# Attention scores as products of 32 rows on four quarters of the array, in place of stacked products fed by copies

## The chip, the core and the metric

The kernel runs on one core of one Trainium2 chip. The time is the device time of one execution in microseconds (us), as the median of three runs. The core has a matrix engine (TensorE, PE in the profile; its weight loads are a row of their own, PEld), a vector engine (DVE), a scalar engine (ACT), a general engine (POOL), and SP, which mostly issues DMAs. Matrix products go to PSUM, which the kernel uses as eight banks of 512 float32 values on each of 128 partitions. The program gives each engine one row of instructions, in the order of the text described below.

## The reference

Two layers of a transformer on `x` of 2 batches x 1024 tokens x 256 channels, with a context of 64 rows per batch. After each layernorm there is a residual step:

```
x += xattn0(ln(x), ctx)   # 16 heads of 16 channels; q, k, v; softmax over the 64 keys; then relu MLP 256-512-256
x += ffn0(ln(x), ...)     # 8 experts, top 2: relu(x wi + bi + low-rank term of the expert), then wo
x += xattn1(ln(x), ctx)   # one head
x += ffn1(ln(x), ...)     # linear
```

The change is in the first attention alone: `scores = q k / 4`, softmax over the 64 keys, for 16 heads.

## The kernel before

The 2048 tokens are cut into eight halves (n = 0 to 7) of 256 tokens, which stay in SBUF. Every piece of work on a half is a generator ("stream"): `q`n makes the queries, `a`n the scores and exponentials, `v`n the product with the values, `m` the MLP, `e`, `d` and `t` the head, the upper and the lower product of the experts, and `o`n the second layer. `m`, `e` and `d` go by blocks of one or two halves (`BLOCKS`). Other streams load and scale the weights (`ld`, `sk`, `ky`, `w0` and so on), and `pe` issues products of zeros that nobody reads. One long text, `ORDER`, lists the steps: each token advances its stream to the next `yield`, and so fixes the order on every engine. A "!" behind a token sets `other[0]`, which lets the helpers (`copy`, `times`, `plus`, `relu`, `two`) take VectorE in place of ScalarE or GpSimd for that step.

Float32 precision is reached by splitting an operand into two float16 parts, high and low, and adding three products: high by high, high by low, low by high (`mm3`, L187).

A half's attention before the change. `att_q` turns the normalised tokens, multiplies them by the query weights, and leaves `qT`, high and low, with the channels on 128 partitions: 8 heads of 16 channels in each of two chunks c. Three DMAs (L540) copy `qT` into `qp`, so that on 96 partitions a pair of heads has its high part, its low part and its high part again below each other; there are four pairs per chunk. The keys lie in `kp` in the same way (high, high, low; L369). One product over 96 rows thus adds all three terms. `att` first makes the scores with tokens on partitions (L557: 16 products of 128 columns a half, each four of them one bank) and takes the largest value of each head on VectorE (L564, four instructions). L571, L574 and L576 subtract a constant and split the maxima into two float16 parts, L579 turns them, `copy` moves them to SBUF, and a DMA (L584) puts them as four more rows into `qp`. The second product (L595, 8 of 256 columns) runs over 100 rows, with keys on partitions, and so yields the scores less their maximum. ScalarE takes the exponential twice (L603 in float32 and L607 in float16; with "!" VectorE copies instead, L605), and `two` (L171) makes the low part. `att_out` (L624) multiplies by the values.

PSUM is one pool of eight banks for all streams (`p_tile`); SBUF scratch tiles come in three sizes, 4, 2 and 1 KB per partition, with the counts in `SLOTS`.

## Time and profile before

| what | value |
|---|---|
| median of three runs | 313.85 us (312.57 to 315.66) |
| the profiled execution: its time, its span | 314.17 us, 312.2 us |
| PE busy | 284.8 us (91%), 2504 products |
| DVE busy | 260.0 us (83%), 774 instructions |
| ACT, POOL busy | 155.8 us (50%), 162.8 us (52%) |
| DMA | 25.38 MB in 53324 packets |
| first product L557; first and last product L595 | at 36.2 us; at 49.7 and 134.1 us |
| first product of the experts (`xT` by `wi`) | at 115.3 us |

The span runs from the first to the last instruction of the program; the time is taken around it, 1.97 us more here. A row of the profile names line, engine, operation and tiles, then busy time, mean duration, and the idle time of the engine ahead of it. The durations of neighbouring products overlap in the timeline; so the distance from start to start, not the duration, says what a product takes of the engine.

### The profile page before, as it was taken

Reading aid. Unit: us, or ns where it says so; the run is one execution under the profiler, and the core shown is the slowest. Engines: PE = TensorE matmul, PEld = TensorE weight load, DVE = VectorE, ACT = ScalarE, POOL = GpSimd, SP = SyncE. Lnnn points to the kernel's source line nnn. Section 1 sums busy time; section 2 is a strip of 40 time slices with the busy share of each in tenths; the row PEclk is TensorE's granted clock in tenths of the full one; section 3 lists DMA queues with packets and bytes.
Section 4 is the critical chain, followed back from the end, with each engine's and each line's share of the span. In section 5 each row is a group of like instructions: output and inputs, shape, how many; then the busy total and the mean of one; then the engine's idle time right before and its main releaser. Section 6 shows DMA issues by size and latency. Waiting matters only on the chain. (4 is left out here: it accounts for less than half of the span.)

```text
span 312.2 us, 6880 instructions
## 1 busy us (share of the span) xinstructions
PE 284.8 (91%) x2504; PEld 208.9 (67%) x2504; DVE 260.0 (83%) x774; ACT 155.8 (50%) x347; POOL 162.8 (52%) x211
## 2 busy tenths in 40 slices
PE   8799979887969799999989989999998999989785
PEld 2455648675958378886876856547765788878563
DVE  3759997999968999995998799699688879979685
ACT  1686486986867855468123531230436244253251
POOL 3583384797765657644624534240735643545441
PEclk9699987998988999999999999999999999999799
DMA  7996988245230013313133203210033121224844
GB/s 249 351 323 154 206 133 118 41 93 50 55 69 2 4 34 38 69 34 69 32 64 59 52 1 72 41 34 11 0 36 76 37 42 36 42 44 95 119 120 149
DMA packets 53324, 25.38 MB, mean 81 GB/s; under 512 B 44838, under 2 KB 49702, under 8 KB 53292
## 3 DMA queue, kind: packets, MB, share of 16 engines
q1 hardware_dynamic: 52732, 24.17, 37.6%
q10 hardware_dynamic: 560, 0.79, 0.8%
q8 instruction: 19, 0.31, 0.4%
q14 instruction: 13, 0.11, 0.1%
HBM read 8.50 MB, written 2.10 MB: 34 GB/s over the span
## 5 line engine op out<-in xcount | busy, mean ns | idle before, releaser
L187 PEld LDWEIGHTS <-h 128*128 128x128 f16 x576 | 54.6, 98 | 11.8 <-issue 2.1
L171 POOL TENSOR_TENSOR h<-r,h 128x256 f16<-128x256 f32 (+1 forms) x33 | 27.4, 830 | 50.9 <-DVE h L148 23.9
L187 PE MATMUL n<-wo_h,h 128*128 128x256 f16 x256 | 44.7, 273 | 0.7 <-POOL h L171 0.7
L187 PE MATMUL n<-uT,lb_h 128*128 128x256 f16 (+1 forms) x192 | 42.3, 308 | 2.4 <-DVE r L166 1.2
L187 PE MATMUL n<-xT,wi_h 128*128 128x256 f16 (+1 forms) x192 | 41.6, 308 | 1.0 <-DVE r L822 0.6
L171 POOL TENSOR_TENSOR e<-e,e 128x512 f16<-128x512 f32 x27 | 31.5, 1171 | 10.1 <-DVE e L605 5.2
L187 PE MATMUL n<-wo_l,h 128*128 128x256 f16 x128 | 34.9, 273 | 0.0
L168 ACT ACTIVATE r<-n,cols 128x256 f32<-128x256 f32 (+1 forms) x33 | 18.0, 548 | 26.1 <-PE n L187 24.7
L171 POOL TENSOR_TENSOR x<-xn,x 128x512 f16<-128x512 f32 x19 | 22.9, 1208 | 15.0 <-ACT x L150 8.7
L187 PE MATMUL n<-xT,wi_l 128*128 128x256 f16 (+1 forms) x96 | 29.6, 308 | 0.0
L187 PE MATMUL n<-uT,lb_l 128*128 128x256 f16 (+1 forms) x96 | 29.6, 308 | 0.0
L199 DVE BATCH_NORM_STATS2 stats<-x 128x6 f32<-128x256 f32 x64 | 24.8, 415 | 4.6 <-DMA x<-in_x_dram 4.3
L150 ACT CAST h<-r 128x256 f16<-128x256 f32 (+1 forms) x21 | 9.7, 463 | 36.8 <-DVE r L822 36.8
L822 DVE SCALAR_TENSOR_TENSOR r<-n,nbi,r 128x256 f32<-128x256 f32 (+1 forms) x48 | 27.0, 564 | 0.7 <-PE n L187 0.7
L206 POOL TENSOR_TENSOR rstd<-rstd,mhalf 128x2 f32<-128x2 f32 (+2 forms) x32 | 22.9, 717 | 6.6 <-DVE rstd L205 4.5
L187 PEld LDWEIGHTS <-lb_h 128*128 128x128 f16 x192 | 18.6, 98 | 11.3 <-issue 3.8
L248 ACT ACTIVATE xn<-x,nm,rstd 128x256 f32<-128x256 f32 x28 | 15.3, 592 | 21.0 <-DVE nm L244 18.3
L1131 PE MATMUL n<-warm 128*128 128x512 f16 x80 | 24.3, 457 | 1.2 <-DVE warm L1135 1.2
L564 DVE TENSOR_REDUCE mm<-n 128x8 f32<-128x512 f32 x32 | 22.1, 690 | 3.7 <-PE n L557 2.2
L187 PEld LDWEIGHTS <-wi_h 128*128 128x128 f16 x192 | 18.4, 98 | 9.0 <-issue 0.8
L187 PE MATMUL n<-aw_h,h 128*128 128x256 f16 x128 | 22.9, 273 | 1.2 <-DVE h L171 1.1
L603 ACT ACTIVATE e<-n,sinv 128x512 f32<-128x512 f32 x32 | 22.0, 690 | 3.0 <-PE n L595 2.6
(260 smaller groups left out, 702.2 us busy)
## 6 DMA issues: line engine op xcount, KB each, us to landing
qp<-qT SPq DMA_DIRECT2D x24, 128.0 KB, 4.3
x<-in_x_dram SPq DMA_DIRECT2D x7, 256.0 KB, 4.7
out_dram<-x SPq DMA_DIRECT2D x7, 256.0 KB, 2.4
raw<-in_aw_dram SPq DMA_DIRECT2D x2, 512.0 KB
raw<-in_wo_dram SPq DMA_DIRECT2D x2, 512.0 KB, 8.1
raw<-in_wi_dram SPq DMA_DIRECT2D x2, 512.0 KB
raw<-in_lb_dram SPq DMA_DIRECT2D x1, 512.0 KB
cw<-in_cw_dram SPq DMA_DIRECT2D x2, 256.0 KB, 5.4
```

Source lines behind the costliest of these rows:

```text
L150: s.copy(dst, src)
L168: s.activation(dst, src, AF.Relu, bias=bias)
L171: (v if other[0] else g).tensor_tensor(dst, x, y, op)
L187: nc.tensor.matmul(pm, lhsT=x, rhs=y, start=start and i == 0, stop=stop and i == 2, skip_group_check=True,)
L199: v.bn_stats(stats[:, t, :], xt)
L206: g.tensor_tensor(rs, rs, mhalf[:, 0:k], ALU.pow)
L248: s.activation(xn[:, t], xt, AF.Identity, bias=nm[:, t : t + 1], scale=rstd[:, at + t : at + t + 1])
L564: v.tensor_reduce(mx[:, :, :, c, t].rearrange("q j p -> q p j"), pm.rearrange("q (p j m) -> q p j m", j=2, m=M), AX.X, ALU.max,)
L603: s.activation(e, pm, AF.Exp, scale=sinv)
L822: v.scalar_tensor_tensor(r1, pa, nbi[:, f : f + 1], r1, ALU.max, ALU.add)
L1131: nc.tensor.matmul(pm, lhsT=warm[:, 0:P], rhs=warm, start=True, stop=True)
```

## The change

The copies between partitions go. Each quarter of the array (32 rows) now holds one pair of heads as `qT` already has it, and the three terms are three products that add up in PSUM.

- `att_q` ends with `qT`; the three copies into `qp` are gone, and so are the three copies into `kp`.
- The keys are two tiles `kd` (high and low) on the same partitions as `qT`; for each of the two heads of a pair the other head's channels are zeroed by multiplying with a mask (`heads`, a column of the input).
- First pass: 48 products of 32 rows and 128 columns a half, in two steps. Four neighbours in the order go to four quarters and four banks. Four maxima instructions follow, one per bank.
- The maxima are split into the tile `ms`, one of two that stay and are zeroed once; the subtraction of the constant is gone, and the exponential gets it as a bias (`raised`).
- Two transposes in place of one, one copy `mT`, no DMA.
- Second pass: 24 products of 32 rows and 256 columns into four banks (one per pair, both chunks), in two steps, then 8 more with a fixed selection matrix `sel` that subtract the maxima. Exponentials as before, one pair of heads and both chunks each.
- `SLOTS` changes, and `ORDER` is a new text: 1500 steps in place of 1548, which is five fewer for each `a` and one fewer for each `q`; every other stream has as many steps as before, in other places and with "!" at other places.

```diff
--- before.py
+++ after.py
@@ -41,12 +41,8 @@
 HTOP = 2.0**15
 USC = 2.0**-8
 MROW = 2048.0
-STOP = 2.0**25
 DMIN = -87.3365
-
-PK = 3 * 32
-PKS = PK + 4
-SHIFT = 40.0
+SHIFT = 10.0
 
 BLOCKS = ((0,), (1,), (2, 3), (4, 5), (6,), (7,))
 
@@ -59,51 +55,50 @@
 
 
 ORDER = """
-l2 ky st pe pe pe q2 q2 q2 l4 q4 q4 q4 q4 l3 q3 l0 pe pe pe pe pe l7! lq ld ld! sk ld sc sc q3 q3 q7 q3! l1 pe
-pe pe pe q7 w0 sk sk pe q0 sk st q7 q7 q4! q0 pe q4 w0 q0 q0 q7! q7 sc sc q0! q1 wq q1 q1 l5 q5 q5 q5 lv q0 q1
...
+st l0! pe q0 q0 q0 l7! q7 q0! q7 q7 l3! q3 q3 pe pe pe ld q0! ld! ld! st pe pe pe pe pe pe pe q3 pe pe q7 q7!
+q7 q0 l1 q1 q1 q1 q0 pe pe lq sk sc sc q3 q3 q0 pe pe pe pe pe sk sk sk q1 q1 pe pe q1 sc sc wq q1 q3 l2 q2 q2
+q2 q2! l5 q5 q5 pe pe q5 pe pe q5 l4 q4 q4 q4 sk q2! q2 w0 w0 s1 s1 s1 sb s1 sk ky ky! ky ky! w5 w5 wq q4 q4!
...
@@ -125,7 +120,7 @@
     work = ctx.enter_context(tc.tile_pool(name="work", bufs=1))
     psum = ctx.enter_context(tc.tile_pool(name="psum", bufs=1, space=bass.MemoryType.PSUM))
 
-    SLOTS = {"k4": 11, "k2": 22, "k1": 25}
+    SLOTS = {"k4": 8, "k2": 25, "k1": 31}
     BANKS = 8
 
     def c_tile(shape, name, dt=F32):
@@ -310,7 +305,7 @@
 
     akT = w_tile([P, DC, P], "akT", "k1")
 
-    cq, ck, sinv, shift, vsc, hk = (c_tile([P, 1], k) for k in ("cq", "ck", "sinv", "shift", "vsc", "hk"))
+    cq, ck, sinv, vsc, hk = (c_tile([P, 1], k) for k in ("cq", "ck", "sinv", "vsc", "hk"))
 
     def setup_scales():
 
@@ -355,26 +350,20 @@
 
     def setup_keys():
 
-        kdh, kdl = (w_tile([P, DC, B, 2, M], k, "k1", F16) for k in ("kdh", "kdl"))
-        g.memset(kdh, 0.0)
-        g.memset(kdl, 0.0)
+        ckj = s_tile([P, 2], "ckj", bufs=1)
+        v.tensor_scalar(ckj, heads, ck, None, ALU.mult)
         yield
         for j in range(2):
-            r = slice(j * M, (j + 1) * M)
-            src = akT[r].rearrange("p c (b m) -> p c b m", b=B)
-            times(kdh[r, :, :, j], src, ck[r])
-            v.scalar_tensor_tensor(kdl[r, :, :, j], src, ck[r], kdh[r, :, :, j], ALU.mult, ALU.subtract)
-        yield
-        for t, src in enumerate((kdh, kdh, kdl)):
-            nc.sync.dma_start(
-                out=kp[t * 32 : t * 32 + 32].rearrange("q p c b j m -> q p (c b j m)"),
-                in_=src.rearrange("q c b j m -> q (c b j m)"),
+            src = akT.rearrange("p c (b m) -> p c b m", b=B)
+            times(kd[0][:, :, :, j], src, ckj[:, j : j + 1])
+            yield
+            v.scalar_tensor_tensor(
+                kd[1][:, :, :, j], src, ckj[:, j : j + 1], kd[0][:, :, :, j], ALU.mult, ALU.subtract
             )
             yield
 
         v.tensor_tensor(sinv, cq, ck, ALU.mult)
         yield
-        v.tensor_scalar(shift, sinv, SHIFT, STOP, ALU.mult, ALU.min)
         v.reciprocal(sinv, sinv)
         yield
         v.tensor_scalar(sinv, sinv, 1.0 / DH**0.5, None, ALU.mult)
@@ -518,7 +507,7 @@
         yield from deviation(tiles(n), dev)
         y = turned_tile(1)
         yield from normalised(tiles(n), dev, 0, y[:, 0], n not in FIRST)
-        qT = [w_tile([P, DC, TH], "qT", "k1", F16) for _ in range(2)]
+        qT = qs[n] = [w_tile([P, DC, TH], "qT", "k1", F16) for _ in range(2)]
         pm = p_tile([P, DC, TH])
         for hc in range(DC):
             for c in range(DC):
@@ -535,80 +524,76 @@
                 qT[1][:, hc], pm[:, hc], abq[:, hc : hc + 1], qT[0][:, hc], ALU.add, ALU.subtract
             )
         yield
-        qp = qs[n] = w_tile([P, 4, DC, TH], "qp", "k4", F16)
-        for t, i in ((0, 0), (2, 0), (1, 1)):
-            nc.sync.dma_start(
-                out=qp[t * 32 : t * 32 + 32].rearrange("q p c t -> q p (c t)"),
-                in_=qT[i].rearrange("q c t -> q (c t)"),
-            )
-        yield
-
     def att(n):
         b = n // HB_PER_B
-
-
-        qp = qs.pop(n)
-        mm = p_tile([P, 2, 32], name="mm")
-        mx, m32 = mm[:, 0].rearrange("q (j p c t) -> q j p c t", j=2, p=4, c=DC), mm[:, 1]
+        qT = qs.pop(n)
+        terms = ((0, 0), (0, 1), (1, 0))
+
+
+
+        mx = p_tile([P, 2, 4, DC * 2], name="mm")
+        pms = [p_tile([P, 2, DC, P]) for _ in range(4)]
+        for t in range(2):
+            for c in range(DC):
+                for i, (x, y) in enumerate(terms):
+                    for pp in range(4):
+                        r = slice(pp * 32, pp * 32 + 32)
+                        nc.tensor.matmul(
+                            pms[pp][:, t, c], lhsT=qT[x][r, c, t * P : (t + 1) * P],
+                            rhs=kd[y][r, c, b].rearrange("q j m -> q (j m)"),
+                            start=(i == 0), stop=(i == 2),
+                        )
+            yield
+        for pp in range(4):
+            v.tensor_reduce(
+                mx[:, :, pp], pms[pp].rearrange("q t c (j m) -> q t (c j) m", j=2), AX.X, ALU.max,
+            )
+            yield
+        ms = mss[n % 2]
+        v.tensor_scalar(ms[:, :, :, 0], mx, 1.0 / MROW, None, ALU.mult)
+        yield
+        v.scalar_tensor_tensor(ms[:, :, :, 1], ms[:, :, :, 0], -MROW, mx, ALU.mult, ALU.add)
+        yield
+
+        pms = [p_tile([P, DC, TH]) for _ in range(4)]
         for c in range(DC):
-            for t in range(2):
-                pm = p_tile()
+            for i, (x, y) in enumerate(terms):
                 for pp in range(4):
+                    r = slice(pp * 32, pp * 32 + 32)
                     nc.tensor.matmul(
-                        pm[:, pp * P : pp * P + P],
-                        lhsT=qp[0:PK, pp, c, t * P : (t + 1) * P],
-                        rhs=kp[0:PK, pp, c, b].rearrange("q j m -> q (j m)"),
-                        start=True, stop=True,
+                        pms[pp][:, c], lhsT=kd[y][r, c, b].rearrange("q j m -> q (j m)"),
+                        rhs=qT[x][r, c], start=(c == 0 and i == 0), stop=False, skip_group_check=True,
                     )
-                yield
-                v.tensor_reduce(
-                    mx[:, :, :, c, t].rearrange("q j p -> q p j"),
-                    pm.rearrange("q (p j m) -> q p j m", j=2, m=M), AX.X, ALU.max,
-                )
-                yield
-
-        ms = s_tile([P, 2, 2, 32], "ms", F16)
-        v.tensor_scalar(m32, mm[:, 0], shift, None, ALU.subtract)
-        yield
-        m2 = m32.unsqueeze(1).to_broadcast([P, 2, 32])
-        v.tensor_scalar(ms[:, :, 0], m2, 1.0 / MROW, None, ALU.mult)
-        yield
-        v.scalar_tensor_tensor(ms[:, :, 1], ms[:, :, 0], -MROW, m2, ALU.mult, ALU.add)
-        yield
-        pt = p_tile([P, P], F16, "t")
-        nc.tensor.transpose(pt, ms.rearrange("q a i m -> q (a i m)"), ident16)
-        yield
-        mT = w_tile([64, P], "mT", "k1", F16)
-        copy(mT, pt[0:64])
-        yield
-        nc.sync.dma_start(out=qp[PK:PKS].rearrange("q p c t -> q (p c t)"), in_=mT)
-        yield
-
-        es[n] = []
+            yield
+        pt = p_tile([P, 2, P], F16, "t")
+        for t in range(2):
+            nc.tensor.transpose(pt[:, t], ms[:, t].rearrange("q p a i -> q (p a i)"), ident16)
+        yield
+        mT = w_tile([P, TH], "mT", "k1", F16)
+        copy(mT, pt.rearrange("p t q -> p (t q)"))
+        yield
         for c in range(DC):
-            ee = []
-            es[n].append(ee)
-            for p2 in range(2):
-                pm = p_tile()
-                for i in range(2):
-                    pp = p2 * 2 + i
-                    nc.tensor.matmul(
-                        pm[:, i * TH : i * TH + TH],
-                        lhsT=kp[0:PKS, pp, c, b].rearrange("q j m -> q (j m)"),
-                        rhs=qp[0:PKS, pp, c], start=True, stop=True,
-                    )
-                yield
-                e = w_tile([P, TB], "e32", "k2")
-                e1, e2 = (w_tile([P, TB], k, "k1", F16) for k in ("e1", "e2"))
-                s.activation(e, pm, AF.Exp, scale=sinv)
-                if other[0]:
-                    v.tensor_copy(e1, e)
-                else:
-                    s.activation(e1, pm, AF.Exp, scale=sinv)
-                yield
-                ee += [(e1[:, i * TH : i * TH + TH], e2[:, i * TH : i * TH + TH]) for i in range(2)]
-                two(e2, e, e1, ALU.subtract)
-                yield
+            for pp in range(4):
+                r = slice(pp * 32, pp * 32 + 32)
+                nc.tensor.matmul(
+                    pms[pp][:, c], lhsT=sel[r, c], rhs=mT[r], start=False, stop=(c == DC - 1), skip_group_check=True,
+                )
+        yield
+        es[n] = [[], []]
+        for pm in pms:
+            e = w_tile([P, DC * TH], "e32", "k2")
+            e1, e2 = (w_tile([P, DC * TH], k, "k1", F16) for k in ("e1", "e2"))
+            pm = pm.rearrange("p c t -> p (c t)")
+            s.activation(e, pm, AF.Exp, bias=raised, scale=sinv)
+            if other[0]:
+                v.tensor_copy(e1, e)
+            else:
+                s.activation(e1, pm, AF.Exp, bias=raised, scale=sinv)
+            yield
+            for c in range(DC):
+                es[n][c].append((e1[:, c * TH : c * TH + TH], e2[:, c * TH : c * TH + TH]))
+            two(e2, e, e1, ALU.subtract)
+            yield
 
     def att_out(n):
         b = n // HB_PER_B
@@ -1045,12 +1030,15 @@
     awk, awv = (w_tile([P, DC, D], k, "k2") for k in ("awk", "awv"))
     bv2 = w_tile([P, 2 * D], "bv2", "k2")
     abv_bc = bv2[:, 0:D]
-    kp = c_tile([P, 4, DC, B, 2, M], "kp", F16)
+    kd = [c_tile([P, DC, B, 2, M], f"kd{i}", F16) for i in range(2)]
+    sel = c_tile([P, DC, P], "sel", F16)
+    mss = [c_tile([P, 2, 4, 8, DC * 2], f"ms{i}", F16) for i in range(2)]
+    raised = c_tile([P, 1], "raised")
     gb_bc = c_tile([P, NE], "gb_bc")
-    cols = c_tile([P, P + 20 + NE + 1], "cols")
+    cols = c_tile([P, P + 20 + NE + 3], "cols")
     ident, bcol = cols[:, 0:P], cols[:, P : P + 20]
     first = cols[:, P + 20 : P + 20 + NE]
-    valw = cols[0:2, -1:]
+    heads, valw = cols[:, -3:-1], cols[0:2, -1:]
     abk, abq, ab1, cbk, cbq, bi = (
         bcol[:, i:j] for i, j in ((0, 2), (2, 4), (4, 8), (8, 10), (10, 12), (12, 20))
     )
@@ -1138,6 +1126,9 @@
         g.memset(ones, 1.0)
         g.memset(orow.bitcast(F32), 1.0)
         g.memset(crow.bitcast(F32), 0.0)
+        g.memset(raised, SHIFT)
+        for i in range(2):
+            g.memset(mss[i], 0.0)
         yield
         copy(ident16, ident)
         yield
@@ -1145,7 +1136,7 @@
 
     streams = {
         "ld": loads(), "lq": load2("awq", awq_raw),
-        "ls": load2("shrow", kp[PK:PKS].rearrange("q p c b j m -> q (p c b j m)")),
+        "ls": load2("sel", sel),
         "lg": load3("gb", gb_bc), "lw": load3("bv2", bv2), "lv": load4(),
     } | {f"l{n}": load1(n) for n in range(XB)}
     streams |= {"pe": warming(), "st": start(), "sc": setup_scales(), "sk": setup_scales_k(), "wq": setup_awq(), "ky": setup_keys(), "va": setup_vals()}
@@ -1192,22 +1183,18 @@
     col = lambda x: x.reshape(-1, P).T
     f32 = np.float32
 
-    def pair(w):
-
-        return w.reshape(-1, DC, 4, 32).swapaxes(2, 3).reshape(w.shape)
-
     r = {"x": i["x"]}
     r["ctxw"] = np.concatenate(
-        [ctx_rows(ctxd), ctx_rows(pair(i["L0_xattn_Wk"])), ctx_rows(i["L0_xattn_Wv"])], axis=2
+        [ctx_rows(ctxd), ctx_rows(i["L0_xattn_Wk"]), ctx_rows(i["L0_xattn_Wv"])], axis=2
     )
     bcol = np.concatenate(
-        [col(pair(i["L0_xattn_" + k])) for k in ("bk", "bq")] + [col(i["L0_xattn_b1"])]
+        [col(i["L0_xattn_" + k]) for k in ("bk", "bq")] + [col(i["L0_xattn_b1"])]
         + [col(i["L1_xattn_" + k]) for k in ("bk", "bq")] + [col(i["L0_ffn_bi"])], axis=1
     )
     r["gb"] = i["L0_ffn_gate_b"]
     r["brow"] = np.stack([np.stack([i["L0_xattn_b2"], i["L0_ffn_bo"]]), np.zeros((2, D), f32)])
     r["bv2"] = np.concatenate([i["L0_xattn_bv"], i["L1_xattn_bv"]])
-    r["awq"] = _rows(pair(i["L0_xattn_Wq"]), np)
+    r["awq"] = _rows(i["L0_xattn_Wq"], np)
     r["aw1"] = _rows(i["L0_xattn_W1"], np)
     r["aw2"] = _rows(i["L0_xattn_W2"], np)
     la = i["L0_ffn_lora_A"].reshape(NE * R, D)
@@ -1221,13 +1208,16 @@
     )
     r["gw"] = _rows(i["L1_ffn_weight"].T, np).reshape(P, DC, D)
     r["dis"] = np.concatenate([i["L1_ffn_disha"]] * 2)
-    sh = np.zeros((4, 2, M), np.float16)
-    for k in range(4):
-        sh[k, k % 2] = -1.0 if k // 2 else -MROW
-    r["shrow"] = np.tile(sh.reshape(4, 2 * M), (1, 4 * DC * 2))
+
+    sel = np.zeros((4, 8, 2, 2, 2, 2, M), np.float16)
+    for c in range(2):
+        for j in range(2):
+            sel[:, 0, c, j, c, j], sel[:, 1, c, j, c, j] = -MROW, -1.0
+    r["sel"] = sel.reshape(P, 2, 2 * M)
+    heads = np.arange(P)[:, None] // DH % 2 == np.arange(2)
     w = np.ones((P, 1), f32)
     first = np.tile(np.arange(NE, 0, -1, dtype=f32), (P, 1))
-    r["cols"] = np.concatenate([np.eye(P, dtype=f32), bcol, first, w], axis=1)
+    r["cols"] = np.concatenate([np.eye(P, dtype=f32), bcol, first, heads.astype(f32), w], axis=1)
     return r
```

## The prediction

> **What bounds the kernel now.** I read the page first, then the busy time by stretches, then pieces of the timeline for what one product takes, then the waits.
>
> ```profile
> PE 284.8 (91%) x2504; PEld 208.9 (67%) x2504; DVE 260.0 (83%) x774; ACT 155.8 (50%) x347; POOL 162.8 (52%) x211
> ```
>
> ```profile
> 20.00:40.00 20.00, 19.55 (x133) 12.38 (x132) 18.18 (x58) 13.35 (x30) 8.98 (x8) 1.00 0.98 181
> 40.00:60.00 20.00, 17.50 (x154) 12.80 (x153) 17.26 (x45) 16.20 (x34) 13.55 (x19) 0.83 0.71 106
> 60.00:80.00 20.00, 16.25 (x230) 13.13 (x226) 19.02 (x49) 15.90 (x31) 17.05 (x16) 0.91 0.38 57
> 80.00:110.00 30.00, 25.34 (x299) 19.73 (x297) 24.86 (x73) 22.25 (x44) 19.25 (x23) 0.94 0.16 34
> 110.00:290.00 180.00, 174.07 (x1533) 131.87 (x1534) 155.00 (x464) 70.92 (x169) 85.69 (x107) 1.00 0.26 44
> 290.00:312.20 22.20, 15.21 (x117) 10.81 (x115) 15.46 (x45) 7.54 (x19) 7.46 (x14) 0.92 0.49 133
> ```
>
> The columns are PE, PEld, DVE, ACT, POOL, the granted clock, the DMA share and GB/s. Two regimes are to be seen. From 110 to 290 us PE is busy 174 of 180 us. Before, from 20 to 110, DVE is busy 79.3 of 90 us, and PE less than it looks, since busy time contains overlapping ends. What a product takes is seen in the timeline:
>
> ```profile
> 58.25 0.76 PE L624 MATMUL n<-v,e 128*128 128x34 f16 x24
> ...
> 85.77 0.61 PE L557 MATMUL n<-kp,qp 96*128 96x128 f16 x8
> ...
> 86.54 0.38 PE L187 MATMUL n<-xT,aw_h 128*128 128x256 f16 x2
> 86.76 0.27 PE L187 MATMUL n<-xT,aw_l 128*128 128x256 f16 x1
> ```
>
> 24 products of 34 columns last 0.76 us and one alone 0.177, so the distance is (0.76 - 0.18) / 23 = 25 ns. For 128 columns it is (0.61 - 0.22) / 7 = 56 ns, for 256 columns 0.38 - 0.27 = 0.11 us (109 ns in long rows). Counted at such distances, PE works only 49 of the 70 us from 40 to 110, but 172 of the 180 from 110 to 290, and 11.6 of the last 22.2. So **DVE leads until about 110 us, PE from there**, and PE has some 21 us free in the stage where most of the attention lies.
>
> ```profile
> DVE vblk L402 <- POOL rstd L206: 2.6, 1, 2.6
> DVE mT L148 <- PE t L579: 2.4, 1, 2.4
> DVE mm L564 <- PE n L557: 2.2, 4, 1.4
> ```
>
> These are the longest of DVE's waits from 20 to 120 us. All its idle time from 20 to 110 is 90 - 79.3 = 10.7 us: no order can win more there, unless DVE gets less to do.
>
> **The copies.**
>
> ```profile
> qp<-qT SPq DMA_DIRECT2D x24, 128.0 KB, 4.3
> ```
>
> 24 copies of queries at 4.3 us to landing go, three of keys, and eight of maxima. The first is issued at 26.8 us, among weight loads (the DMA share is 0.98 there), and the first score product starts at 36.2. But DVE is busy 18.2 of those 20 us with other steps, so this delay is mostly covered. I count it only through DVE's idle time. SP is no bound: a copy takes it about 0.6 us. The transposing DMAs behind these copies come forward, which nobody on the path waits for by the rows above.
>
> **TensorE.** Before, a half takes 16 x 56 + 8 x 109 ns and one transpose of 56: 1.82 us. Afterwards it has 48 products of 128 columns, 24 + 8 of 256 and two transposes. No row shows products on different quarters, so I bound them. If they don't overlap, 48 x 56 + 32 x 109 + 112 = 6.29 us, which is +4.5 us a half. If four overlap fully, a group of four takes the longer of four starts at 25 ns and one product: 12 x 100 + 8 x 109 + 112 = 2.18 us, or +0.36 us. Nothing below that is possible, as the starts alone take it. I take the second, since neighbours go to four quarters and four banks and have nothing to wait for in each other.
>
> The Trainium skill, "TensorE: Matmul & The Clock Gate", section "Measured speedup vs the span model", gives 3.07 times for four products of 32 rows and 512 columns, not 4. No row here shows it; applied to 256 columns, an estimate from that page is 142 ns a group, +0.27 us a half on top.
>
> Between products of 128 rows and of fewer there is a gap. This trace shows it once in plain view, in float32, where a product of 64 rows follows two of 128:
>
> ```profile
> 19.21 0.38 PE L393 MATMUL n<-awv,ctxd 128*128 128x256 f32 x1
> ...
> 19.43 0.38 PE L393 MATMUL n<-awv,ctxd 128*128 128x256 f32 x1
> ...
> 19.74 0.48 PE L393 MATMUL n<-awv,ctxd 64*128 64x256 f32 x1
> ```
>
> Like follows like after 0.22 us, unlike after 0.31: 0.09 us a change. In the new order the 40 steps that issue 32-row products stand in 24 stretches, so 48 changes, 4.3 us or 0.54 a half. Bounds: 0, and 0.16 us a change, the part of a duration beyond its distance (273 - 109 ns), which makes 7.9 us.
>
> The Trainium skill, "TensorEngine Tiling (Array Packing)", section "Key Properties", speaks against the change here: changing the tiling mode drains the engine. The gap of 0.09 us agrees with a partial drain; a full one would be the upper bound just given.
>
> Together +0.9 us a half. Where it lies matters: in the new order six halves have both passes, and `a6` its first, before PE has done 80 us of work (I summed both orders step by step at the rows' durations), that is in the stage with 21 us free. There 6 x 0.9 = 5.4 us are hidden. `a7` and the second pass of `a6` stand among the experts' products: **+1.8 us** for two halves.
>
> **VectorE.** L571 goes: 8 x 255 ns = -2.0 us. The mask product of `ckj` comes and `shift` goes, about 0.2 us each. The four maxima a half stay as they are (8 results from 512 values). The "!" moves work to DVE inside `a`: 12 casts of 567 ns in place of 5 and 10 differences of 926 ns in place of 5, +8.6 us; other streams get fewer. Summed over all the steps of both orders DVE has 1.5 us more, but at the point where PE has done 76 to 80 us of work it stands at 96 in place of 97: **-1 us** in the stage that it leads. ACT (+5 us) and POOL (-7) have room at 50%.
>
> **The order.** Before, the second MLP block ends at 100.6 us (second row of L682), where my sum stands at 74 us of DVE steps; the experts' products, which fill PE, begin at a sum of 90, at 115.3 us. The new order begins them at a sum of 74. PE is idle 3 us between 100 and 110, of which I take **-2 us**. The idle of DVE: the mT wait of 2.4 and the mm waits of 2.2 are tied to the steps that are rebuilt, and the starts behind copies go. Bounds are 0 and -10.7; I take **-4 us**, nearest to those two rows' 4.6. The order of the first 20 us, where DVE is busy 10.2, is new as well (`l0` and `q0` first in place of `l2`); bounds -3 and +3, the size of its longest wait there (4.0 us for `x`), taken as 0.
>
> **Banks.** A half's first pass now holds five of eight PSUM banks until the maxima are read, the second four until the exponentials; before it was two and one. Counting tiles that are open along the two orders, the attention part rises from 1 to 2.4 banks on average to 3 to 5. The bounds are 0 and, if PE stands still while each half's bank is emptied (four maxima of 0.69 us, less the half of them that other banks cover), 1.4 us a half, +11 us. I take **+1.5 us**, for one such stall in the PE-led part.
>
> **The sum.** On the profiled execution's own 314.17 us (span 312.2, 1.97 around it): +1.8 - 1 - 2 - 4 + 1.5 = -3.7. That execution lies 0.3 us above the median of 313.85, so the forecast for a median is 310.2, say **310 us**.
>
> **Rivals.** *Banks turn into the bound.* The products of the first pass come as a block of 48 that needs four free banks at once, and everything behind them on PE, MLP and expert products too, waits. The price is the 1.4 us a half above, 11 us, from the point where fewer than four banks are free when the block's turn comes: 310 + 11 = 321 us, slower than before. For it: open banks rise to the pool's eight at twelve steps of the new order, before to seven at most. Against it: PE has 21 us free in that stage.
>
> *The quarters don't overlap.* Then six halves take 6 x (4.5 + 0.5) = 30 us more in a stage with 21 free, +9, and two halves 10 in the stage that PE leads: 314 + 19 = 333 us. For it: the trace has no such product. Against it: nothing that a neighbour waits for.
>
> *Nothing is won.* The copies were covered and DVE does the same work: -1 - 2 + 1.8 + 1.5, so 314 us. For it: only 4.6 us of DVE's waits name the steps concerned.
>
> **How the numbers follow.** The forecast's case, 302 to 312, has 0.46; the banks 0.26 (316 to 326); no overlap 0.12 (325 to 340); nothing won 0.16 (311 to 317). About 1% is what a measurement of this kernel can tell from no change. The forecast's case gives 0.41 of faster and 0.05 of same; nothing won 0.13 of same and 0.03 of slower; the banks 0.02 of same and 0.24 of slower; the last all slower: 0.41, 0.20, 0.39. The range leaves out no overlap beyond its lower end and a little at the fast end: 301, which is all of DVE's 10.7 us and part of the first 20 us, to 326, the banks' bound with the full drain. The forecast's own range is 302 to 312.
>
> **What would show it.** Rows of 32-row products: 24 of them in some 0.8 us (25 ns apart) if quarters overlap, 1.5 us if not. The gap at a stretch's edge: 0.09 us. DVE from 20 to 100 us busier than 88%. The first expert product near 100 us. PE idle behind DVE's maxima or ScalarE's exponentials would show the banks. The prediction is wrong if DVE's idle grows in the first 110 us, since a new order for the whole kernel can lose there what the copies gave, or if PE idles in the stretch from 110 us on.

## The result, and the profile after

The changed kernel takes **323.43 us** (median of four runs, 321.28 to 323.99) beside 313.37 us for the kernel before on the same chip: a ratio of **1.030, 95% interval 1.024 to 1.037, slower**. The profiled execution took 321.28 us with a span of 319.1. The forecast was 310; the range of 301 to 326 holds the result, the direction was wrong. Medians below are over all of a run's executions; ratios and intervals leave out those more than 1.5% above a kernel's fastest (four of E10's ten below, two of E14's ten).

The page's line of busy times, after the change:

```profile
PE 285.5 (89%) x2960; PEld 203.6 (64%) x2960; DVE 263.7 (83%) x764; ACT 164.5 (52%) x360; POOL 157.9 (49%) x202
```

TensorE is busy as long as before, in 456 more products; VectorE has 3.7 us more, ScalarE 8.7 more. Nothing in this line explains 7 us of span. The stretches do (PE, PEld, DVE, ACT, POOL, then the granted clock, the DMA share and GB/s):

```profile
20.00:40.00 20.00, 17.87 (x209) 11.34 (x207) 17.46 (x61) 15.58 (x37) 8.25 (x8) 0.91 0.71 165
40.00:60.00 20.00, 16.36 (x255) 10.93 (x255) 19.17 (x43) 16.21 (x32) 14.51 (x17) 1.00 0.15 28
60.00:80.00 20.00, 13.25 (x209) 9.38 (x208) 16.36 (x34) 10.98 (x22) 10.47 (x13) 0.91 0.08 15
80.00:110.00 30.00, 27.39 (x386) 19.86 (x387) 26.42 (x81) 21.08 (x40) 17.42 (x19) 0.89 0.11 19
110.00:290.00 180.00, 168.47 (x1606) 123.17 (x1604) 149.40 (x431) 77.83 (x172) 84.43 (x99) 1.00 0.25 43
290.00:319.10 29.10, 24.10 (x221) 19.47 (x218) 22.50 (x73) 12.84 (x37) 12.17 (x21) 1.00 0.46 109
```

From 20 to 110 us VectorE is busy 79.4 of 90 us, as before (79.3). TensorE lost: 13.25 us of 20 in 60 to 80 (16.25 before), and 168.47 of 180 from 110 on (174.07). The last stretch is 7 us longer, but fuller.

Busy time contains overlapping ends, so I also counted TensorE's idle time from starts: the distance from one product's start to the next, less what the product takes, wherever this is over 0.15 us. (Such counts move by 1 us or so with what is taken for a product.) It is **21.4 us from 20 to 110 us (15.9 before) and 14.1 from 110 to 290 (7.8 before)**. In products done, with the products of zeros left out, TensorE stands 4.4 us behind the kernel before at 110 us (56.5 against 60.9 us of work) and 10.9 behind at 150 us (88.4 against 99.3). Some of that comes back at the end, where the kernel before had more waits of its own.

The products themselves went better than forecast. The rows of the timeline (start, duration, engine, line, tiles, form, number):

```profile
37.43 0.85 PE L541 MATMUL n<-kd,qT 32*128 32x128 f16 x48
...
85.75 0.27 PE L182 MATMUL n<-xT,awq_h 128*128 128x256 f16 x1
85.86 0.27 PE L182 MATMUL n<-xT,awq_l 128*128 128x256 f16 x1
86.07 0.83 PE L563 MATMUL n<-qT,kd 32*128 32x256 f16 x24
86.83 0.28 PE L570 MATMUL t<-ident,ms 128*128 128x128 f16 x2
```

One such product lasts 0.214 us at 128 columns and 0.268 at 256, so the first and the last of the 48 start 0.64 us apart, those of the 24 start 0.56 us apart: 58 and 112 ns a group of four, hardly more than one product alone. The gap at the edges is here too: 0.21 us into the stretch where like follows like after 0.11, and 0.20 out of it (86.83 - 86.63) where 0.11 is the product's own.

TensorE's longest wait of the first 110 us is of another kind:

```profile
64.31 0.70 DVE L548 TENSOR_REDUCE mm<-n 128x8 f32<-128x512 f32 x1
64.42 0.28 PE L563 MATMUL n<-qT,kd 32*128 32x256 f16 x2
64.79 1.89 POOL L166 TENSOR_TENSOR h<-h,h 128x256 f16<-128x256 f32 x2
64.92 0.58 DVE L1087 SCALAR_TENSOR_TENSOR guw<-raw_u,SC,guw 128x16 f16<-128x16 f32 x1
65.06 0.83 PE L563 MATMUL n<-qT,kd 32*128 32x256 f16 x22 [0.36 <-DVE mm L548]
65.41 0.74 DVE L1087 SCALAR_TENSOR_TENSOR aw_l<-raw,SC,aw_h 128x512 f16<-128x512 f32 x1
66.08 0.76 DVE L143 CAST h<-h 128x256 f16<-128x256 f32 x1
...
68.58 1.50 DVE L548 TENSOR_REDUCE mm<-n 128x8 f32<-128x512 f32 x2
69.33 0.27 PE L570 MATMUL t<-ident,ms 128*128 128x128 f16 x2 [3.44 <-DVE mm L548]
...
71.38 0.64 PE L182 MATMUL n<-aw_h,h 128*128 128x256 f16 x2
...
73.92 0.38 PE L182 MATMUL n<-aw_h,h 128*128 128x256 f16 x2
```

This is the trace of the changed kernel with VectorE and GpSimd beside TensorE. The transposes L570 belong to half 2. Their `ms` was done at 60.9 us; they need a bank of PSUM, and the next bank comes free with the third maxima instruction of half 4 (68.58). (That it is the bank is read from the code; E14 below tests it.) That instruction stands eight others behind the second (64.31) in VectorE's row. TensorE waits 3.44 us, and everything behind the transposes with it. Two more things show. Products of 256 columns start 0.22 us apart at 71.38 (two last 0.64 us, one alone 0.42 there) and 0.11 at 73.92 (0.38 - 0.27): the clock is halved for a while after the wait. And a cast that usually lasts 0.29 us takes 0.76 at 66.08, while GpSimd works.

From 110 us on the waits are scattered. The largest, from the timeline:

```profile
144.69 0.27 PE L182 MATMUL n<-uT,lb_l 128*128 128x256 f16 x1
147.26 0.52 PE L182 MATMUL n<-gk,xT 128*128 128x64 f16 x12 [2.30 <-DMA xT<-x]
```

### The profile page after: what moved, and what is told of

It reads as the page before. It is cut to its first block, busy times and chain, and to the rows that moved or that the text cites. A ratio compares the mean times of both kernels' runs of the same rounds, so it can differ in the third digit from the quotient of the medians.

```text
span 319.1 us, 7679 instructions
## 1 busy us (share of the span) xinstructions
PE 285.5 (89%) x2960; PEld 203.6 (64%) x2960; DVE 263.7 (83%) x764; ACT 164.5 (52%) x360; POOL 157.9 (49%) x202
## 4 chain that ended last, share of the span: by engine, by line
PE 49%; DVE 30%; ACT 6%; issue 5%; DMA 5%; POOL 3%; ACTq 1%; DVEq 0%; POOLq 0%
PE n L182 39%; PE n L1119 3%; DVE mm L548 3%; DVE r L807 2%; DMA cols<-in_cols_dram 2%; DMA uT<-us 2%; DVE xn L235 2%; DVE stats L194 2%; PE n L609 1%; DVE h L166 1%; DVE e L166 1%; DVE qT L523 1%; DVE r L161 1%; PE n L635 1%; DVE us L166 1%
## 5 line engine op out<-in xcount | busy, mean ns | idle before, releaser
L166 POOL TENSOR_TENSOR h<-r,h 128x256 f16<-128x256 f32 (+1 forms) x28 | 24.4, 873 | 33.6 <-ACT h L145 14.1
L166 POOL TENSOR_TENSOR e<-e,e 128x512 f16<-128x512 f32 x22 | 26.7, 1225 | 24.0 <-DVE e L589 19.0
L166 POOL TENSOR_TENSOR x<-xn,x 128x512 f16<-128x512 f32 x20 | 23.7, 1194 | 15.7 <-ACT x L145 10.9
L201 POOL TENSOR_TENSOR rstd<-rstd,mhalf 128x2 f32<-128x2 f32 (+2 forms) x32 | 23.2, 726 | 14.2 <-DVE rstd L200 12.2
L243 ACT ACTIVATE xn<-x,nm,rstd 128x256 f32<-128x256 f32 x33 | 18.0, 591 | 23.4 <-DVE nm L239 22.1
L163 ACT ACTIVATE r<-n,cols 128x256 f32<-128x256 f32 (+1 forms) x33 | 17.0, 523 | 20.6 <-PE n L182 18.5
L145 ACT CAST h<-r 128x256 f16<-128x256 f32 (+1 forms) x26 | 12.1, 468 | 27.8 <-DVE r L807 27.8
L587 ACT ACTIVATE e<-n,raised,sinv 128x512 f32<-128x512 f32 x32 | 23.9, 778 | 3.3 <-PE n L578 3.3
L182 PE MATMUL n<-aw_h,h 128*128 128x256 f16 x128 | 24.0, 284 | 0.0
L166 POOL TENSOR_TENSOR h<-h,h 128x256 f16<-128x256 f32 (+1 forms) x20 | 18.5, 930 | 10.5 <-ACT h L145 4.6
```

The lines of the kernel that those rows point to most:

```text
L145: s.copy(dst, src)
L163: s.activation(dst, src, AF.Relu, bias=bias)
L166: (v if other[0] else g).tensor_tensor(dst, x, y, op)
L182: nc.tensor.matmul(pm, lhsT=x, rhs=y, start=start and i == 0, stop=stop and i == 2, skip_group_check=True,)
L201: g.tensor_tensor(rs, rs, mhalf[:, 0:k], ALU.pow)
L243: s.activation(xn[:, t], xt, AF.Identity, bias=nm[:, t : t + 1], scale=rstd[:, at + t : at + t + 1])
```

## The experiments

Two theories. **The order's**: the new products are as good as the old, and the new `ORDER` fits the queues worse. **The products'**: four or five banks held at a time, 48 changes of mode and the rebuilt maxima cost time in any order. Ratios below are to the kernel before, run on the same chip, with 95% intervals. Labels have no meaning beyond their order; there is no fourth.

### The two parts crossed

E1 has products of 32 rows and no copies in the order of the kernel before. That order doesn't leave four banks free, so two quarters are served at a time, in two banks:

```diff
-        pms = [p_tile([P, 2, DC, P]) for _ in range(4)]
...
+            pms = [p_tile([P, 2, DC, P]) for _ in range(2)]
...
+                        for k in range(2):
+                            r = slice((2 * g + k) * 32, (2 * g + k) * 32 + 32)
...
+        for g in range(2):
+            pms = first(g)
+            yield
```

> The 32-row products without any copies, but in the order of the kernel before: each of its steps is kept, steps that have nothing left to do drop out, and two banks (two quarters at a time) take the place of four, since four banks a pass don't fit that order. By counts, TensorE has 24 x 56 + 16 x 109 + 110 ns = 3.2 us a half, 1.4 us more than before, 11 us in all, most of it in the stage with 21 us free. Theory A (the new order is what costs): 310 to 316 us. Theory B (the new products and their banks cost, whatever the order): 319 to 326 us.

Measured: 324.91 us, ratio 1.036 (1.034 to 1.039). The number is in the range of the products' theory, but the run doesn't decide: two neighbours take 56 and 109 ns where four did, so the scores take 24 x 56 + 16 x 109 + 112 ns = 3.2 us a half in place of 1.65, and there are more stretches, each with its two changes. TensorE's idle time from 20 to 110 us is only 8.0 us in this order, with VectorE busy 72.4 of the 90.

E2 is the reverse: the stacked products and the copies in the new order.

```diff
-    SLOTS = {"k4": 11, "k2": 22, "k1": 25}
+    SLOTS = {"k4": 13, "k2": 25, "k1": 31}
 ORDER = """
-l2 ky st pe pe pe q2 q2 q2 l4 q4 q4 q4 q4 l3 q3 l0 pe pe pe pe pe l7! lq ld ld! sk ld sc sc q3 q3 q7 q3! l1 pe
+st l0! pe q0 q0 q0 l7! q7 q0! q7 q7 l3! q3 q3 pe pe pe ld q0! ld! ld! st pe pe pe pe pe pe pe q3 pe pe q7 q7!
...
```

> The stacked products and all the copies of the kernel before, in the new order: every step of the scores is split back into the steps it came from, in its new place; more SBUF slots (13, 25, 31). Theory A (the order costs): 319 to 332 us, at the upper end if the copies, which the new order leaves no time for, are waited for. Theory B (the products and their banks cost): 311 to 316 us.

Measured: 361.98 us, ratio 1.155 (1.153 to 1.157), beyond what either theory had. TensorE's longest waits of it (us in total, times, longest):

```profile
PE n L595 <- DMA qp<-mT: 19.9, 6, 6.9
```

The new order starts the second pass where a copy of the maxima hasn't landed. It was made for products without copies, and two other waits for DMAs, of 7 us each, come with it. So an order and its products can't be exchanged, and crossing them measures mostly that.

### Single costs of the products

E3 sends neighbours to the same quarter and the same bank, pair by pair, in place of four quarters in turn:

```diff
         for t in range(2):
-            for c in range(DC):
-                for i, (x, y) in enumerate(terms):
-                    for pp in range(4):
+            for pp in range(4):
+                for c in range(DC):
+                    for i, (x, y) in enumerate(terms):
```

> The changed kernel with the loop over pairs of heads outside the loop over terms, so that neighbours go to the same quarter and the same bank. If neighbours on different quarters overlap fully (the trace of the changed kernel has 56 ns for four products of 128 columns, 109 ns for four of 256), the first pass goes from 0.68 to 2.7 us and 24 products of the second from 0.65 to 2.6 us: 4 us a half, 32 us in all, of which some 20 find idle time: 333 to 345 us. If TensorE has room everywhere: 323 to 326 us.

Measured: 320.25 us, ratio 1.022 (1.020 to 1.024; two executions), not slower than the changed kernel, and below both ranges of the expectation. The timeline of E3:

```profile
35.68 1.42 PE L541 MATMUL n<-kd,qT 32*128 32x128 f16 x48
```

48 products start within 1.42 - 0.21 = 1.2 us, 26 ns each, where one after the other would take 48 x 56 = 2.7. So the products didn't come one after the other, as the upper range had assumed, and the run doesn't tell what that would cost. Each half pays 0.57 us more in the first pass, and the time doesn't show it: so much more of the score products costs nothing in this order.

E5 leaves out the constant that the exponential adds (a common factor of a softmax's numerator and denominator):

```diff
-            s.activation(e, pm, AF.Exp, bias=raised, scale=sinv)
+            s.activation(e, pm, AF.Exp, scale=sinv)
```

> The changed kernel with the bias of the exponential left out (each weight is smaller by the same factor, which the softmax divides out; float16 rounding differs). The exponentials took 690 ns before and 778 ns with the bias tensor; if the bias is the cause they go back to 690, 51 x 88 ns = 4.5 us less on ScalarE. If ScalarE's part is on the path: 318 to 321 us; if the order alone counts: 322 to 324 us.

Measured: 320.90 us, ratio 1.027 (1.022 to 1.031). The median lies in the range for ScalarE on the path, but one of the four executions took 324.15 us and the interval overlaps that of the changed kernel: at most it is 2 or 3 us of the 10, and the run doesn't settle whether it is any. The groups of the changed kernel and of E5 (busy us, mean ns of one, idle before):

```profile
L587 ACT ACTIVATE e<-n,raised,sinv 128x512 f32<-128x512 f32 x32 | 23.9, 778 | 3.3 <-PE n L578 3.3
```

```profile
L587 ACT ACTIVATE e<-n,sinv 128x512 f32<-128x512 f32 x32 | 21.1, 689 | 4.1 <-PE n L578 4.0
```

The bias as a tensor costs 89 ns an exponential, 4.5 us for the 51 of them, on an engine that is busy 52% of the span.

### Both orders refitted

What is left is the order itself. E6 keeps the changed kernel's products and refits its `ORDER`; E7 does the same for the kernel before. Steps were moved a little earlier or later, or "!" set or taken away, and a move was kept where the traces' durations, laid one behind the other along the five engines' rows with every wait that the program has, came out shorter. No time in this text is from that sum; the kernels were run.

```diff
 ORDER = """
-st l0! pe q0 q0 q0 l7! q7 q0! q7 q7 l3! q3 q3 pe pe pe ld q0! ld! ld! st pe pe pe pe pe pe pe q3 pe pe q7 q7!
+l0! st pe q0 pe pe pe q0 pe pe pe pe l7 q0 q7 q7 l3! pe ld! q0 q7 lq l1! pe pe ld! q3 q3 pe ld pe pe q0! q3 q7
...
```

> The changed kernel with its products, slots and streams as they are, and its order refitted to the durations and delays of the traces at hand: steps are moved, and 170 of 561 choices of engine are turned over; no step is added or left out. The order's theory (the new order fits the queues worse than the old one fitted its own: PE stood idle 21.4 us in 20-110 and 14.7 us after 110, against 15.9 and 7.8 before) expects at least 15 us of this idle time to go: 297 to 308 us, faster than the kernel before. The products' theory (four or five banks held at a time, 48 changes of mode and the rebuilt maxima cost time in any order) expects 315 to 323 us, since the idle time before the maxima cannot be ordered away.

> The kernel before, with its stacked products and copies, and its order refitted in the same way and for as long (164 of 560 choices of engine turned over). The order's theory expects the two refitted kernels within 4 us of each other, so 296 to 308 us here. The products' theory expects this one at least 7 us under the refitted new products. A third theory, that the order of the kernel before was already fitted and only the new one was not, expects 309 to 315 us here, with the refitted new products below it.

Measured: **E6 304.25 us, ratio 0.968 (0.961 to 0.974); E7 302.62 us, ratio 0.963 (0.957 to 0.969)**. The order's theory is borne out: with the same banks, no fewer changes of mode (56 in the trace against 50) and the same maxima the new products are 3% faster than the kernel before. The third theory, that the order before was already fitted, falls: it had 11 us to give as well. Between the two refitted kernels lie 1.6 us, and the intervals overlap. Each order is one that was found, not the best there is, so I read this as: the products are worth nothing that this comparison can see. (The granted clock wasn't equal: 0.977 to 0.983 in E6, 0.989 to 1.000 in E7; the last section says what that may be worth.)

The windows 20 to 110 and 110 to 290 of E6, then of E7:

```profile
20.00:110.00 90.00, 80.83 (x1195) 56.50 (x1194) 78.16 (x228) 73.26 (x146) 53.37 (x59) 0.92 0.24 50
110.00:290.00 180.00, 176.41 (x1624) 130.48 (x1622) 155.60 (x468) 80.28 (x185) 86.89 (x108) 1.00 0.28 48
```

```profile
20.00:110.00 90.00, 77.34 (x899) 59.14 (x898) 85.29 (x239) 75.89 (x156) 60.32 (x64) 1.00 0.49 92
110.00:290.00 180.00, 173.24 (x1497) 131.38 (x1496) 146.73 (x458) 79.59 (x192) 88.92 (x111) 1.00 0.27 49
```

E6 has 176.4 us of TensorE in the 180, where the changed kernel has 168.5. By starts its idle time is 14.2 us before 110 (21.4) and 5.6 to 290 us (14.1).

### Which stage

E8 refits only the first 530 of the 1500 steps, E9 only those behind them; E13 refits the first 610 of 1548 of the kernel before. As a sample, E9's first changed line:

```diff
-e1 d0! d0 d0 a3! a5 a5 w4! a5 a5 d0 d0 v2 d0 d0 d0! d0 a5 e1 d0 d0! v3 v3 v3 d0! a5 a5 d0 d0 a5 d0! d0 d0 d0!
+e1 d0! d0 d0 a3! a5 a5 w4! a5 a5 d0 d0 v2 d0 d0 d0! d0 a5 e1 d0 d0! v3 v3 v3 d0! a5 a5 d0 d0 a5 d0! d0 v4! d0
```

and those of E8 and E13:

```diff
-st l0! pe q0 q0 q0 l7! q7 q0! q7 q7 l3! q3 q3 pe pe pe ld q0! ld! ld! st pe pe pe pe pe pe pe q3 pe pe q7 q7!
+l7 st pe l0! q0 q0 l3! pe pe q0 pe pe q7 q7 q7 s1 q0 q3 q3 pe pe pe pe pe pe pe pe pe pe pe q3 q0! l1! l4 q7!
...
-l2 ky st pe pe pe q2 q2 q2 l4 q4 q4 q4 q4 l3 q3 l0 pe pe pe pe pe l7! lq ld ld! sk ld sc sc q3 q3 q7 q3! l1 pe
+st l7! l4! pe pe pe pe pe pe pe pe ky l2 q4 l3 q4 q4 ld! q2 q2 pe pe q4 pe pe pe q3 ld! q3 q3 l0 pe q0 q3 lq
```

> The changed kernel, of whose order only the first 530 of 1500 steps are refitted, those that start before some 110 us (325 moved, 37 choices of engine turned over). If the time was lost before 110 us, where the maxima hold the banks, this alone gives back 8 us or more: 300 to 314 us. If it was lost from 110 us on, it gives 317 to 322.

> The changed kernel, of whose order only the steps from the 530th on are refitted (475 moved, 121 choices of engine turned over). If the time was lost before 110 us, 314 to 322 us; if it was lost from 110 us on, where PE stood idle 14.7 us against 7.8 before, 306 to 314 us.

> The kernel before, of whose order only the first 610 of 1548 steps are refitted, those that start before some 110 us (388 moved). If the order before was better fitted to this stage than the new one, it gives back clearly less than the 12.6 us of the changed kernel: 306 to 312 us. If both orders had equal room before 110 us, and the new one lost elsewhere: 299 to 304.

| steps refitted | changed kernel | kernel before |
|---|---|---|
| those before 110 us | 310.81, ratio 0.990 (0.986 to 0.994) | 303.97, ratio 0.972 (0.965 to 0.979) |
| those from 110 us on | 318.48, ratio 1.014 (1.008 to 1.021) | not run alone |
| all | 304.25, ratio 0.968 | 302.62, ratio 0.963 |

Before 110 us the changed kernel had 12.6 us to give and the kernel before 9.4; E13's 303.97 is at the upper end of the second range of its expectation, so the two had nearly equal room there. From 110 us on the changed kernel gained 5.0 when only those steps were refitted (E9 lies in the range of a loss before 110 us, and yet it gains), and lies 6.6 below E8 when all are; the kernel before gained only 1.4 beyond E13. Like with like, then, the new order is worse by 12.6 - 9.4 = 3.2 us before 110 us and by 6.6 - 1.4 = 5.2 from there, together the 8.4 us that E6 and E7 leave to the order. Each refit was made by itself (E8 and E9 aren't the two parts of E6), and the intervals are about 2 us either way, so which share is larger isn't shown. No single stage holds the loss.

### Which part of the order, and one wait alone

E10 moves no step and turns over 49 choices of engine among the first 530; E11 moves only their attention steps (`a0` to `a5`), E12 only the others. First lines:

```diff
-st l0! pe q0 q0 q0 l7! q7 q0! q7 q7 l3! q3 q3 pe pe pe ld q0! ld! ld! st pe pe pe pe pe pe pe q3 pe pe q7 q7!
+st l0! pe q0 q0 q0 l7 q7 q0 q7 q7 l3! q3 q3 pe pe pe ld q0! ld! ld st pe pe pe pe pe pe pe q3 pe pe q7 q7 q7
...
-q5 sc ky q0 q0! q0 pe va lv va lw q4! va va ky a0 va w1 ky w2 w1 w2 w6 w6 cr q1 w3 w3 ky a0 q7 pe pe lg w4 w4
+q5 sc ky q0 q0! q0 pe va lv va lw q4! va va ky va w1 ky w2 w1 w2 w6 w6 cr q1 w3 w3 ky q7 pe pe a0 lg a0 a0 a0
...
-st l0! pe q0 q0 q0 l7! q7 q0! q7 q7 l3! q3 q3 pe pe pe ld q0! ld! ld! st pe pe pe pe pe pe pe q3 pe pe q7 q7!
+l7! st l0! pe pe pe pe pe pe pe pe pe pe pe pe pe pe pe l1 q0 ld! lq q0 q0 q1 ld! ld l3! sc q1 q7 q7 q0 q0! lv
```

> The changed kernel with no step moved; among the first 530 steps 49 choices of engine are turned over (31 to VectorE's side or back inside the streams a, m, e and d, the rest in the setup). Theory C (the loss before 110 us is the place of the attention steps, whose products and transposes hold TensorE behind the maxima: 8.0 us of idle behind L548) expects little here, 319 to 323 us. Theory D (the stage is led by VectorE, and what counts is how much its queue has to carry before each product, in its own work and in instructions that stand while GpSimd works) expects 5 to 10 us less than the changed kernel: 313 to 318.

> The changed kernel; among the first 530 steps only those of the streams a0 to a5 are moved (106 steps, the mark for the engine goes with 12 of them). Theory C expects most of the 12.6 us that the refit of all 530 steps gave back: 309 to 315 us, with TensorE's idle time behind L548 down from 8 us to 2 or 3. If the place of the attention steps isn't the matter: 318 to 323.

> The changed kernel; among the first 530 steps only those that are not attention steps are moved (281 steps; the mark goes with 24). Theory C expects little: 317 to 323 us. If the misfit is spread over the whole order and any of its parts can give room: 309 to 315, as much as the attention steps alone, and the two together no more than the 12.6 us already seen.

Measured: E10 312.39 us, ratio 0.994 (0.989 to 0.998); E11 309.63 us, 0.987 (0.981 to 0.992); E12 308.59 us, 0.984 (0.979 to 0.989). Each of three quite different rearrangements gives back 11 to 15 us, as much as all of them together in E8. Theory C, that it is the place of the attention steps, isn't needed: E12 leaves these where they are. Theory D's range (313 to 318) was just left on the fast side by E10, so the choice of engine alone is enough too. What all of them have in common is less idle time behind the maxima L548 from 20 to 110 us: 8.0 us in the changed kernel, 2.3 in E10, 4.4 in E11, 4.7 in E12, 2.5 in E8, 2.8 in E6, and 2.1 in the kernel before. That this is the cause isn't shown. These are single traces, and E9, whose first 530 steps are those of the changed kernel, has less of it too: 4.0 us by the profile's list of waits, against 6.6. And E8, E10, E11 and E12 share a second thing: their granted clock was 0.983 to 1.000 in the executions behind the ratios, that of the changed kernel 0.968 to 0.979.

(E10's trace is of an execution of 315.9 us, longer than its median.)

E14 is made to take away the wait shown above alone. Two of the 1500 steps move, the third and the fourth maximum of half 4, up behind the second, ahead of the eight instructions counted above (the expectation says nine):

```diff
-a2 a2 a2 a2 a2 a1 w1 w1 q4 a2 a2 a2 q4 q4 q4 a1! wg s4 m0 m0 q5 q5 m0 m0 q5 cr q5 a4 a4 a4 a4 wg! wg m0 w1 w1!
-m0 m0! wg! a1 m0! q6 q6! q6! m0 m0 m0 m0 m0 m0 m0 a2 a2 a2 a2 a2 a4 a4 a4 w3 a2! a4 m0 m0 q6 m0 a2 a2! a5 a5
+a2 a2 a2 a2 a2 a1 w1 w1 q4 a2 a2 a2 q4 q4 q4 a1! wg s4 m0 m0 q5 q5 m0 m0 q5 cr q5 a4 a4 a4 a4 a4 a4 wg! wg m0
+w1 w1! m0 m0! wg! a1 m0! q6 q6! q6! m0 m0 m0 m0 m0 m0 m0 a2 a2 a2 a2 a2 a4 w3 a2! a4 m0 m0 q6 m0 a2 a2! a5 a5
```

> The changed kernel; only the last two maxima of the half a4 stand earlier, directly behind its first two, ahead of nine instructions of other streams on VectorE. The wait's theory (TensorE's longest wait of the stage, 3.4 us of the transposes L570 for a bank that a4's maxima hold, delays what follows, with the half clock that comes after it) expects 2 to 5 us less than the changed kernel: 318 to 321. If VectorE leads the stage and TensorE's wait costs nothing, 322 to 324.

Measured: 317.36 us, ratio **1.010 (1.006 to 1.013)** where the changed kernel has 1.030 (1.024 to 1.037): about 6 us for two moves, more than the 2 to 5 expected. The same place in the trace of E14:

```profile
65.52 3.09 DVE L548 TENSOR_REDUCE mm<-n 128x8 f32<-128x512 f32 x4
...
68.67 0.27 PE L570 MATMUL t<-ident,ms 128*128 128x128 f16 x2
```

The four maxima run in one piece and the transposes no longer wait. So TensorE's idle time did cost, although VectorE was the busier engine of the stage. In the changed kernel it was 3.4 us of standing and, behind it, 3.4 us at half clock; at this place in E14's trace neither is there. Not all of the 6 us need be this one wait: in the executions of E14 behind its ratio the granted clock was 0.984 to 0.995, in the changed kernel's 0.968 to 0.979. Where the two come closest, E14 took 317.7 and 319.2 us (the profiled one) at 0.984, the changed kernel 321.3 at 0.979: 2 to 4 us. How the 6 us divide between the standing, the half clock behind it and half clocks elsewhere isn't separated.

## Why the prediction was wrong

**What bounds the kernel.** Right as far as it went: VectorE is busy 88% of 20 to 110 us in both kernels, TensorE fills the rest. What was missing is that an engine with 20 us of free time can still be late: TensorE's waits before 110 us weren't taken out of its free time. Nor is VectorE's idle time the most that an order can win there: E11, which only moves steps, won 13.8 us in the changed kernel, whose VectorE is idle 10.6, part of it with the higher clock.

**The copies.** Right that the kernel before covers them. E2 adds that this was the work of its order: with the same copies in another order TensorE waits 19.9 us at L595 alone.

**TensorE.** The overlap was right, and better than assumed: the four starts are 3 to 4 ns apart, not 25, so the starts were no lower bound, and a group of 128 columns takes 56 to 58 ns, not 100. A half takes 12 x 56 + 8 x 109 + 112 ns = 1.65 us, less than the 1.82 before, where the prediction had 2.18. The change of mode was 0.09 us each way, as taken. The term of +1.8 us is not visible: E3 adds 0.57 us a half at no cost. By the measured figures it would have been 2 x (1.65 - 1.82 + 0.54) = 0.7.

**VectorE.** The -1 us isn't to be seen: busy time from 20 to 110 is the same. The 89 ns of the bias on ScalarE were missed; their price is between nothing and 2 or 3 us (E5).

**The order: here it failed.** The prediction took -2 us since the experts' products would begin earlier, and -4 from VectorE's idle time. The first part of the first came true: the first product of `xT` by `wi_h` stands at 102.2 us, forecast near 100, before 115.3. It was worth nothing that shows, since by 110 us TensorE had done 4.4 us less work in all; and E7, which starts these products at 106.5 us, isn't slower than E6, which starts them at 91.7. The start of the filling stage says when some of it is ready, not how much is left. And VectorE's idle time stayed at 90 - 79.4 = 10.6 us. In their place the order cost: (323.43 - 313.37) - (304.25 - 302.62) = **8.4 us** is what the changed kernel lost beyond the difference that stays when both orders are refitted, with some 3 us of doubt by the intervals. That is 14 us from the -6 of the forecast, and the whole error of 13.

**Banks.** The mechanism of the first rival was real, and the +1.5 us taken for it too small: TensorE stood 8.0 us behind the maxima against 2.1 before, and taking one of these waits away gave about 6 us, with the clock that came with it (E14). The result of 323 us lies in the rival's range of 316 to 326. But it isn't a price per half, as the rival's 1.4 us had it: the refitted kernel holds the same banks, waits 2.8 us and takes 304. In the one wait that was taken apart it depended on what VectorE had in its row between a half's second and third maximum. That the stated range holds the result is luck for the same reason: its upper end came from that price per half.

Of the prediction's two signs of being wrong one came, TensorE idle from 110 us on (14.1 us against 7.8); the other, more idle time of VectorE before 110 us, did not (10.6 against 10.7): it was TensorE that lost there. The sign for the banks came too, TensorE idle behind VectorE's maxima. This could have been read off the new order, in which eight instructions stand between the second and the third maximum of a half, and another half's transposes ask for a bank in the meantime.

**The rivals.** "The quarters don't overlap" fell with the first row of the timeline. "Nothing is won" had the products' part right: the terms of the products and banks, +1.8 - 1 + 1.5, are 2.3 us, and E6 against E7 gives 1.6.

What stays open: which of the 49 choices of E10 matter, whether VectorE's shorter row or the shorter standing behind GpSimd (last section) does it, and how much of each gain is the clock. That the one wait (6 us) and the steps from 110 us on (5.0) add up to about the loss of 10 is no proof that these two are the loss, as the order before had room too.

## What to carry to other kernels

When a change comes with a new order for everything, the order is the larger change: cost it by walking each engine's row, not by milestones, and refit both orders before the new instructions are judged. Banks that another engine empties one after the other stay held until each of its instructions comes up in its row; put these together, or whoever waits for the bank pays for everything that stands between. Idle time of TensorE in a stage that another engine leads isn't free: the work it delays comes back when TensorE leads, and here a half clock followed on top.

## What the runs showed of the hardware

**Quarters.** Products on different quarters start 3 to 4 ns apart, and four take as long as one. The Trainium skill, "TensorE: Matmul & The Clock Gate", section "Measured speedup vs the span model", has about 4 ns per tile, and this trace agrees; the same table's 3.07 times, from which the prediction took an estimate of 142 ns a group, isn't what a stream of groups shows here (109 to 112 ns). E3 shows more: even when six neighbours in a row go to one quarter and one bank, 48 products start 26 ns apart on average, less than the 56 of one after the other. Whether those for the next quarter run ahead, or those of one quarter overlap, the trace doesn't tell.

**Half clock.** The clock changes in steps of 3.41 us. The stretches 65 to 70 and 70 to 75 us of the changed kernel, with TensorE's busy time, products, clock, DMA share and GB/s:

```profile
65.00:70.00 5.00, 1.10 (x24) 1.00 0.00 2
70.00:75.00 5.00, 4.94 (x33) 0.66 0.27 52
```

The changed kernel has four such half clocks after the first 20 us, each behind 3.41 us in which TensorE was busy 0.69, 1.49, 1.50 or 2.20 us; four others with 1.72 to 1.89 us busy were not followed by one, so the busy time alone doesn't settle it. The profiled execution of the kernel before has five after its first 20 us, and its mean clock is lower (0.962 against 0.979), so they don't explain why the changed kernel is slower. They do go with the scatter: executions of E10 took 309.6 to 310.0 us at a mean clock of 1.00, 312.0 at 0.994 and 312.8 at 0.989; those of E14 315.0 to 315.5 at 0.995 and 317.0 to 317.4 at 0.989. One stretch of 3.41 us at half clock lowers the mean by 0.005, so each goes with some 1 to 2 us, an estimate from these executions. By it the two or more stretches fewer in E8, E10, E11, E12 and E14 make 2 us or more of their gains, and the 1.6 us between E6 and E7 could be clock alone.

**VectorE beside GpSimd.** The cast at 66.08 us lasted 0.76 us and the work on 16 columns at 64.92 lasted 0.58, both while GpSimd ran the row at 64.79. In E14, at another place, the same work on 16 columns lasted 0.23. Against the usual duration of the same form, some 20 instructions of VectorE lasted about 10 us longer in all from 20 to 110 us in the changed kernel, 14 by 7 before, 12 by 5 in E10 and 13 by 4 in E6. In E14, which is faster, such a count gives as much as in the changed kernel, so this sum doesn't set the time by itself.
